# First sequence's heads by products into row groups, and a new deal of the pieces between attention steps

## Chip, cores and metric

The kernel runs on one core of one Trainium2 chip. Its time is the device time of one execution in microseconds, as the median of the runs of one chip.

## What is computed

Eight sequences of 256 tokens with 128 channels pass through five residual blocks, all in fp32. The change touches the end of the first expert block, the attention block, and the start of the second expert block.

```python
x = L0_attn_x                                     # (8, 256, 128)
x = x + 0.5 * _L0_ffn_ref(_layernorm(x), ...)     # 8 experts, 2 for each token
x = x + _L0_attn_ref(_layernorm(x), w_q, w_k, w_v, w_o)
x = x + 0.5 * _L0_ffn_ref(_layernorm(x), ...)     # the same experts again
x = x + 0.5 * _L1_ffn_ref(_layernorm(x), ...)     # channel mix
x = x + _L1_attn_ref(_layernorm(x), ...)          # gated long convolution
x = x + 0.5 * _L1_ffn_ref(_layernorm(x), ...)

# attention: 16 heads of 8 channels, within each sequence
scores = jnp.einsum('bqhd,bkhd->bhqk', q, k) * 8 ** -0.5
weights = jax.nn.softmax(scores, axis=-1)
out = jnp.einsum('bhqk,bkhd->bqhd', weights, v)
concat @ w_o.T

# experts
h = rmsnorm(x @ W_in.T, in_norm_w)
logits = h @ Wr.T                                 # 2 best of 8, softmax over both
out += gates[:, e:e+1] * rmsnorm(silu(h @ Wg[e].T) * (h @ Wu[e].T) @ Wd[e].T, enorm_w[e])
rmsnorm(out, out_norm_w) @ W_out.T
```

## The kernel before

The 2048 tokens lie as four chunks of four tiles of 128 tokens (`xs`); a chunk is two sequences. The kernel has five stages. The first expert stage routes the tokens (`dispatch`), scatters their rows by expert into HBM (`hs`), and `experts` works through 23 groups of 256 rows, whose results GpSimd scatters into `y2`. In the second stage, attention, each chunk's results are first fetched and added to the tokens (`combine`), and the tokens that are done with attention are already routed for the second expert stage (`dispatch` with f=1, in the parts `LATE`: three chunks, then two times two tiles). Then come the second expert stage and a tail with the other three blocks.

The program fixes by hand the order of instructions on TensorE (PE), VectorE (DVE), ScalarE (ACT) and the DMA queue of SyncE (SP): each engine executes what the code issues to it in the order of the code, and waits in place for what an instruction reads. GpSimd (POOL) is not among these four; its order is made when the program is compiled. So a piece of work that is put between two others also stands between them on every engine that it uses.

**Attention steps.** `attention` runs 32 steps s, one for each sequence b and each group g of four heads (`place`: b, g = divmod(s, 4)), and eight more to drain. A head's 8 channels lie on the first 8 of 32 partitions, a row group; four row groups j hold four heads, and `qs` and `ks` (the halves of `qks`, two buffers, by chunk) have a column block for each g. Row 8 of each row group in `ks` is 1, so that the negated maximum of a query, written in row 8 of `qa`, is subtracted by the product itself. A step issues (L947 and on):

- first half: the products `ps` of `weights(s-2, 1)` with `pm` of `scores(s, 0)` side by side; the exponential `es` of the former (ACT, `power`); `turn_top(s-1)`, which transposes the maxima (`pmt`) and adds them to the queries (`qa`, DVE L851); the pieces `first[s]`; the maximum `m` of `scores(s, 0)` (DVE L839)
- second half: `weights(s-1, 0)` with `scores(s, 1)`, exponential, maximum, `average(s-2)` (products `po` of `es` with the values), then the pieces `second[s]`

`weights` takes its bank pair always from `pz`, so a product waits for the exponential before it. The pieces between take the one bank `sa` ("side").

**Pieces of a chunk before its steps.** `mixing` (from `combine` by way of `combined`): `fetch` (SP: two DMAs), `sums` (cf: DVE, power on POOL), `added` (acc: four tiles by DVE for f=0 and by ACT for f=1, four additions on DVE), `turned` (pan; copy and squares on ACT), `produced` (ori: power on POOL; pout), `update` (x, DVE). Then `norm_sums` (statistics on DVE, power on POOL), `norm_rows` (xn_a, DVE L725), `turn_rows` (pxn_a, copy), `to_heads` (pqk for queries, then for keys; after both a DMA of `qkc` to HBM, L747, and four DMAs, one for each j, from there to the rows of `qks`, L750), `values` (pv). `power_of` is L138, `(x) ** -0.5` on POOL.

The prologue runs all of this for chunks 0 and 1, the second two pieces behind the first; only the last two pieces of chunk 1 are dealt to steps 0 and 1. The pieces of chunk c+1 for c = 1, 2 are dealt to the steps o-2 to o+5, with o = 8c.

**Pieces after.** For each sequence `turn_back`, `turn_heads`, `out_heads` (the output projection, added to x). For each part of `LATE` the pieces of `dispatch`: `turned` (pxt), `half0` and `half1` (pin; copy and squares on ACT), `measured`, `normed` (ri: power on POOL; logits lg on DVE L339; rows hrow scaled on ACT L342), two times `choice` (DVE), `places` (prank; DVE), `rows` (two row scatters for each tile on POOL, L399). They are dealt from step o+12 on; the last two parts come in steps 32 to 37. `table` then counts the groups, and the second expert stage's loads follow.

Of the kernel before, what the change touches and what calls it, by code (L numbers as in the profile page):

```python
# [16 lines left out]
P = 128  # L17
# [28 lines left out]
def macaron_kernel(ctx: ExitStack, tc: tile.TileContext, a: dict, out: bass.AP):  # L46
# [59 lines left out]
    for c in range(1, NCH):  # L106
# [10 lines left out]
    idx_col, onehot, rpe_in, rpe_g, rpe_b, onw, wout_t = pack(  # L117
        "pack3", [2, 1, FEAT, LAYERS * FEAT, LAYERS * FEAT, 1, D]
# [24 lines left out]
    def inv_rms(src, dst, name, eps=rms_eps):  # L143

        n = src.shape[1]
        sq = norm.tile([P, n, D], F32, tag="sq", name=f"sq_{name}")
        nc.scalar.activation(sq, src, AF.Square)
        nc.vector.tensor_reduce(dst, sq, AX.X, ALU.add)
        nc.scalar.activation(dst, dst, AF.Sqrt, bias=eps, scale=1.0 / D)
        nc.vector.reciprocal(dst, dst)  # L150

# [131 lines left out]
    def dispatch(f, i, parts, mp):  # L283
# [45 lines left out]
        def normed():  # L329
# [6 lines left out]
            else:  # L336
                power_of(ri, ri, mhalf.to_broadcast([P, nt]))
            st["lg"] = small.tile([P, nt, E], F32, tag="lg", name=f"lg_{n}")
            nc.vector.tensor_mul(st["lg"], st["u"][:, :, D : D + E], bc_last(ri, E))  # L339
            for t in range(nt):  # L340
                u = st["u"][:, t, 0:D].unsqueeze(1).to_broadcast([P, 2, D])
                nc.scalar.activation(hrow[:, t, :, 0:D], u, AF.Copy, scale=ri[:, t : t + 1])  # L342
# [67 lines left out]
        return turned, *halves, measured, normed, *choices, places, rows  # L410
# [173 lines left out]
    def combine(f, c, gates, y2, mp, work=None, half=None):  # L584

        n = f"f{f}_{c}"
        st = {}
        work = work or (lambda tag, name: norm.tile([P, TPC, D], F32, tag={"A": "acc", "B": "at", "C": "sq"}[tag], name=f"{name}_{n}"))
        half = half or (lambda tag, name: bank(f"{name}_{n}", "side"))

        def fetch():
            st["y"] = mp.tile([P, 2, TPC, ROW], F32, tag="y", name=f"y_{n}", bufs=4 if f else 2)
            for k in range(2):
                r = k * NTOK + c * CT
                nc.sync.dma_start(st["y"][:, k], y2[r : r + CT, :].rearrange("(t p) c -> p t c", p=P))

        def sums():
            y = st["y"]
            st["cf"] = small.tile([P, 2, TPC], F32, tag="cf", name=f"cf_{n}")
            nc.vector.tensor_scalar(st["cf"], y[:, :, :, D], 1.0 / D, RMS_EPS, ALU.mult, ALU.add)  # L600
            half = mhalf.unsqueeze(2).to_broadcast([P, 2, TPC])
            power_of(st["cf"], st["cf"], half)

        def added():
            y, cf = st["y"], st["cf"]
            nc.vector.tensor_mul(cf, cf, gates[:, ts(c, TPC), :].rearrange("p t k -> p k t"))
            acc = work("A", "acc")
            for t in range(TPC):
                scale = cf[:, 0, t : t + 1]
                if f:  # L610
                    nc.scalar.activation(acc[:, t], y[:, 0, t, 0:D], AF.Copy, scale=scale)  # L611
                else:
                    nc.vector.tensor_scalar(acc[:, t], y[:, 0, t, 0:D], scale, None, ALU.mult)
            for t in range(TPC):
# [3 lines left out]
            st["acc"] = acc  # L618

        def turned():  # L620
            acc = st["acc"]
            pt = half("a", "pan")
            for t in range(TPC):
                nc.tensor.transpose(pt[:, ts(t, P)], acc[:, t, :], ident)
            st["at"] = work("B", "at").rearrange("p t d -> p (t d)")
            nc.scalar.copy(st["at"], pt)
            st["ss"] = small.tile([P, TPC], F32, tag="ss", name=f"oss_{n}")
            sq = work("C", "osq")
            for t in range(TPC):
                nc.scalar.activation(sq[:, t], acc[:, t], AF.Square, accum_out=st["ss"][:, t : t + 1])  # L630

        def produced():
            ri = small.tile([P, TPC], F32, tag="ri", name=f"ori_{n}")
            nc.vector.tensor_scalar(ri, st["ss"], 1.0 / D, RMS_EPS, ALU.mult, ALU.add)
            power_of(ri, ri, mhalf.to_broadcast([P, TPC]))
            pp = half("b", "pout").rearrange("p (t d) -> p t d", t=TPC)
            for t in range(TPC):
                nc.tensor.matmul(pp[:, t, :], st["at"][:, ts(t, P)], wout_o, start=True, stop=True)
            st["ri"], st["pp"] = ri, pp

        def update():
            x = xs[c]
            for t in range(TPC):
                nc.vector.scalar_tensor_tensor(
                    x[:, t], st["pp"][:, t], st["ri"][:, t : t + 1], x[:, t], ALU.mult, ALU.add
# [26 lines left out]
    def heads(hp):  # L672
# [26 lines left out]
        def attention(mixing, leaving, filter_ends):  # L699
# [5 lines left out]
            with tc.tile_pool(name="at2", bufs=2, reuse_waits="tile") as a2:  # L705
                lns, normed, flat, qkc, osbs, ccs, cts, ess, tops = ({} for _ in range(9))

                def norm_sums(c):
                    x = xs[c]
                    st = small.tile([P, TPC, 6], F32, tag="ast", name=f"ast_{c}")  # L710
                    mv = small.tile([P, TPC, 2], F32, tag="amv", name=f"amv_{c}")
                    for t in range(TPC):
                        nc.vector.bn_stats(st[:, t, :], x[:, t, :])
                    for t in range(TPC):
                        nc.vector.bn_aggr(mv[:, t, :], st[:, t, :])
                    rs = small.tile([P, TPC], F32, tag="ars", name=f"ars_{c}")
                    nc.vector.tensor_scalar(rs, mv[:, :, 1], LN_EPS, None, ALU.add)
                    power_of(rs, rs, mhalf.to_broadcast([P, TPC]))
                    lns[c] = mv, rs

                def norm_rows(c):
                    mv, rs = lns[c]
# [627 lines left out]
```

## Time and profile before

| | us |
|---|---|
| median of three runs (727.02, 730.21, 735.18) | 730.21 |
| profiled execution | 732.74 |
| its span | 731.00 |

| Stretch of the span, us | length | PE busy | ACT busy | DVE busy | granted clock |
|---|---|---|---|---|---|
| 209.67 to 236.15: first combined rows to first scores | 26.48 | 13.92 | 7.13 | 11.43 | 0.65 |
| 236.15 to 246.74: to the first `qa` | 10.59 | 8.19 | 0.59 | 2.45 | 0.50 |
| 246.74 to 284.07: to the eighth `qa` | 37.33 | 31.87 | 15.76 | 22.58 | 0.84 |
| 284.07 to 428.25: to the 32nd `qa` | 144.18 | 122.08 | 75.22 | 96.97 | 0.92 |
| 428.25 to 457.15: to the places of the last two tiles | 28.90 | 18.73 | 8.15 | 11.30 | 0.50 |

Over the whole span PE is busy 574.2 us (79%), DVE 373.3 (51%), ACT 272.7 (37%) and POOL 210.5 (29%). The instruction of `qa` with number k belongs to step k, so the distance between two of them is the length of a step. A row of the timeline gives start, duration, engine, line, operation, the tile written and the tiles read, their shapes and the count; in brackets stands how long the engine was idle before, and what ended that. The granted clock is the share of full speed that TensorE had. Products of 32x256 in the steps last 0.48 us (the first of a group) at clock 1.00 and 0.80 at 0.50.

### The profile page before, as it was taken

How to read it: one execution, taken by the hardware profiler on the slowest of the kernel's cores; microseconds unless marked ns; L12 is line 12 of the kernel's file. 1: busy time of each engine (PE TensorE's matmuls, PEld its weight loads, DVE VectorE, ACT ScalarE, POOL GpSimd, SP SyncE). 2: the span in 40 equal slices, each digit the busy share in tenths (PEclk: the TensorE clock that was granted, in tenths of full speed). 3: DMA queues.
4: the chain of work that ended last, by engine and by line, in shares of the span. 5: the costliest groups of instructions: out<-in, count | busy, mean ns of one | idle time of the engine just before them, and what ended most of it. 6: DMA issues, size and time to landing. Idle time of an engine off the chain costs nothing. (4 is left out here: it accounts for less than half of the span.)

```text
span 731.0 us, 11632 instructions
## 1 busy us (share of the span) xinstructions
PE 574.2 (79%) x4023; PEld 447.7 (61%) x4023; DVE 373.3 (51%) x1109; ACT 272.7 (37%) x664; POOL 210.5 (29%) x217
## 2 busy tenths in 40 slices
PE   3533999999945789998979684199999981779985
PEld 2432988899833445564545343189999971457863
DVE  4661655444343357687557445334444431566564
ACT  3531232223222145574554432022332322765343
POOL 1573456433331001001400442213343343321010
PEclk9999999999966599999999765599999996679998
DMA  5128456666233400030210000756666524000001
GB/s 189 37 82 227 166 181 184 199 195 206 63 87 77 67 2 1 2 59 1 69 21 1 30 30 15 202 160 211 203 196 212 190 62 116 1 0 2 1 14 44
DMA packets 41515, 69.55 MB, mean 95 GB/s; under 512 B 5291, under 2 KB 31698, under 8 KB 41328
## 3 DMA queue, kind: packets, MB, share of 16 engines
q1 hardware_dynamic: 35312, 59.26, 28.1%
q0 software_dynamic: 4992, 8.48, 3.6%
q10 hardware_dynamic: 1152, 1.06, 0.6%
q8 instruction: 32, 0.52, 0.3%
q14 instruction: 27, 0.22, 0.1%
HBM read 55.05 MB, written 15.56 MB: 97 GB/s over the span
## 5 line engine op out<-in xcount | busy, mean ns | idle before, releaser
L555 POOL DMA_INDIRECT y<-yrow_f,idx_f x92 | 90.2, 981 | 160.7 <-issue 153.5
L819 PE MATMUL ps<-qa,qk 32*128 32x256 f32 x512 | 82.2, 443 | 24.1 <-ACT es L856 21.9
L399 POOL DMA_INDIRECT hs<-hrow,posi_f x64 | 61.9, 967 | 109.1 <-issue 48.5
L839 DVE TENSOR_REDUCE m<-pm 128x4 f32<-128x1024 f32 x64 | 77.2, 1220 | 29.2 <-PE pm L802 29.2
L537 PE MATMUL py_f<-w_f,hg_f 128*128 128x128 f32 x736 | 90.2, 276 | 2.4 <-DVE yrow_f L548 2.4
L537 PEld LDWEIGHTS py_f<-w_f,hg_f 128*128 128x128 f32 x736 | 88.6, 192 | 4.9 <-DVE yrow_f L548 2.7
L517 PE MATMUL pg_f<-ht_f,w_f 128*128 128x256 f32 x368 | 90.6, 391 | 1.2 <-issue 0.6
L856 ACT ACTIVATE es<-ps 128x1024 f32<-128x1024 f32 x64 | 65.5, 1023 | 67.2 <-PE pm L802 33.9
L530 DVE TENSOR_TENSOR hg_f<-pu_f,sg_f 128x1024 f32<-128x1024 f32 x46 | 56.3, 1225 | 61.6 <-PE pu_f L526 61.6
L526 PE MATMUL pu_f<-ht_f,w_f 128*128 128x256 f32 x368 | 87.4, 381 | 0.0
L802 PE MATMUL pm<-qk 32*128 32x256 f32 x512 | 81.8, 445 | 7.0 <-DMA qk<-heads 7.0
L819 PEld LDWEIGHTS ps<-qa,qk 32*128 32x128 f32 x512 | 49.4, 206 | 47.0 <-ACT es L856 39.4
L519 ACT ACTIVATE sg_f<-pg_f 128x1024 f32<-128x1024 f32 x46 | 47.1, 1024 | 77.3 <-PE pg_f L517 77.3
L517 PEld LDWEIGHTS pg_f<-ht_f,w_f 128*128 128x128 f32 x368 | 68.7, 197 | 10.0 <-issue 1.0
L526 PEld LDWEIGHTS pu_f<-ht_f,w_f 128*128 128x128 f32 x368 | 66.9, 191 | 7.3
L547 ACT ACTIVATE ysq_f<-py_f 128x128 f32<-128x128 f32 x92 | 24.6, 274 | 122.8 <-PE py_f L537 122.8
L802 PEld LDWEIGHTS pm<-qk 32*128 32x128 f32 x512 | 49.1, 207 | 10.2 <-issue 8.2
L511 DVE TENSOR_SCALAR ht_f<-pht_f,pack 128x256 f32<-128x256 f32 x46 | 22.2, 484 | 50.4 <-PE pht_f L509 50.4
L548 DVE TENSOR_TENSOR yrow_f<-py_f,w_f 128x256 f32<-128x256 f32 x46 | 19.6, 426 | 52.8 <-ACT ysq_f L547 52.8
L509 PE MATMUL pht_f<-ident,hst_f 128*128 128x128 f32 x92 | 18.4, 283 | 31.2 <-DMA hst_f<-hs 31.2
L866 PE MATMUL po<-es,v 128*32 128x256 f32 x512 | 40.1, 428 | 0.1
L138 POOL TENSOR_TENSOR cf_f<-cf_f,mhalf 128x8 f32<-128x8 f32 x8 | 13.1, 1643 | 88.1 <-DVE cf_f L600 88.1
(243 smaller groups left out, 826.2 us busy)
## 6 DMA issues: line engine op xcount, KB each, us to landing
w_f<-in_wall_dram SPq DMA_DIRECT2D x46, 832.0 KB
hst_f<-hs SPq DMA_DIRECT2D x46, 129.0 KB
y_f<-y SPq DMA_DIRECT2D x16, 258.0 KB
heads<-qkc SPq DMA_DIRECT2D x4, 512.0 KB
qk<-heads SPq DMA_DIRECT2D x16, 128.0 KB
pack<-in_pack_dram SPq DMA_DIRECT2D x1, 1729.0 KB
y<-yrow_f,idx_f POOLq DMA_INDIRECT x92, 4.5
hs<-zero ACTq DMA_DIRECT2D x8, 129.0 KB
```

What stands on the lines that cost most here:

```text
L399: ins = nc.gpsimd.indirect_dma_start(out=hs, out_offset=bass.IndirectOffsetOnAxis(ap=st["posi"][:, t, k : k + 1], axis=0), in_=hrow[:, t, ...
L517: nc.tensor.matmul(pg[:, k, :], w[t][:, ts(k, P)], ht[t], start=True, stop=True)
L519: nc.scalar.activation(sg, pg, AF.Silu)
L526: nc.tensor.matmul(pu[:, k, :], w[t][:, DFF + k * P : DFF + k * P + P], ht[t], start=True, stop=True)
L530: nc.vector.tensor_mul(hg[t], pu, sg)
L537: nc.tensor.matmul(py[:, s, :], hg[t][:, k, ts(s, P)], w[t][:, 2 * DFF + k * D : 2 * DFF + k * D + D], start=(k == 0), stop=(k == NFC - 1),)
L555: ins = nc.gpsimd.indirect_dma_start(out=y2, out_offset=bass.IndirectOffsetOnAxis(ap=idx[:, s : s + 1], axis=0), in_=yrow[:, s, :], in_off ...
L802: nc.tensor.matmul(sc[:, jj, i, :], qs[c][r, g, col + i * P : col + (i + 1) * P], ks[c][r, g, col : col + S], start=True, stop=True,)
L819: nc.tensor.matmul(sc[:, jj, i, :], ks[c][r, g, col + i * P : col + (i + 1) * P], tops[s][r, :], start=True, stop=True,)
L839: nc.vector.tensor_reduce(m, sc, AX.X, ALU.max, negate=True)
L856: nc.scalar.activation(es, sc, AF.Exp, scale=scale)
L866: nc.tensor.matmul(po[32 * j : 32 * j + 32, :], vs[c][:, (b % 2) * 2 + i, (g % 2) * (H // 2) + (g // 2) * 4 + j, :], ess[s, j // 2][:, j % ...
```

## The change

1. **First sequence.** The prologue no longer works on chunks 0 and 1, but on the two sequences of chunk 0 (tiles 0, 1 and 2, 3), the second two pieces behind the first. All pieces take a range of tiles. The queries and keys of the first sequence go to no DMA: `heads_of_first(g)` multiplies with the weights' columns from 8g on, so that group g's heads fall on the first 8 rows of each row group, and writes them to `ks` (DVE: times a mask of those rows, plus the row of ones) and to `qs` (ACT: times the mask). Group 0 is made in the prologue, groups 1 to 3 in steps 0 to 2. The second sequence's heads take the DMAs, from step 0.
2. **Chunk 1** is combined, normalized and projected in steps 0 to 6, as the later chunks are in theirs. For all chunks `sums` to `values` now stand in steps o-1 to o+6 instead of o-2 to o+5; both products of `to_heads` stand at the end of step o+5, where they stood in step o+4.
3. **Engines.** The first factor of `added` is scaled on ACT for f=0 too; `norm_rows` goes from DVE to ACT (with an offset computed on DVE).
4. **Routing for the second expert stage.** `normed` is split into `normed` (power), `logits` and `scaled`, which can be dealt apart; all pieces are dealt out anew, and those of the last two parts stand in steps 32 to 34. The first expert stage and the tail issue what they issued.

```diff
-        return turned, *halves, measured, normed, *choices, places, rows
+        if f == 0:
+            return turned, *halves, measured, both(normed, logits, scaled), *choices, places, rows
+        return turned, *halves, measured, normed, logits, scaled, *choices, places, rows
...
-                if f:
-                    nc.scalar.activation(acc[:, t], y[:, 0, t, 0:D], AF.Copy, scale=scale)
-                else:
-                    nc.vector.tensor_scalar(acc[:, t], y[:, 0, t, 0:D], scale, None, ALU.mult)
+            for t in own:
+                nc.scalar.activation(acc[:, t], y[:, 0, t, 0:D], AF.Copy, scale=cf[:, 0, t : t + 1])
...
+                def heads_of_first(g):
+                    m = P - HD * g
+                    pp = bank(f"pqk1_{g}", "side").rearrange("p (i s) -> p i s", i=2)
+                    for i in range(2):
+                        w = (wq_t, wk_t)[i][:, HD * g : P]
+                        nc.tensor.matmul(pp[0:m, i, :], w, flat[0, 0][:, 0:S], start=True, stop=True)
+                    nc.vector.tensor_scalar(
+                        ks[0][0:m, g, 0:S], pp[0:m, 1, :], lanes8[0:m], onehot[0:m], ALU.mult, ALU.add
+                    )
+                    nc.scalar.activation(qs[0][0:m, g, 0:S], pp[0:m, 0, :], AF.Copy, scale=lanes8[0:m])
...
                     if c < NCH - 2:
+                        n = c + 1
                         at(o + 12, None, turned)
-                        at(o + 13, None, half0, measured)
-                        at(o + 15, None, half1)
-                        at(o + 16, None, None, normed_)
-                        at(o + 18, None, choice0)
-                        at(o + 19, None, choice1)
-                        at(o + 20, None, None, places)
+                        at(o + 13, None, half0)
+                        at(o + 14, half1, measured)
+                        at(o + 15, None, normed_)
+                        at(o + 16, None, logits)
+                        at(o + 17, None, choices[0], partial(scaled, [0, 1]))
+                        at(o + 19, None, partial(scaled, [2, 3]))
+                        at(o + (20 if n < NCH - 2 else 18), None, choices[1])
+                        at(o + (21 if n < NCH - 2 else 19), None, places)
                         for i in range(TPC):
-                            at(o + 21 + i, None, partial(rows, [i]))
+                            at(o + (21 if n < NCH - 2 else 20) + i, None, partial(rows, [i]))
                     elif c == NCH - 2:
-                        at(o + 12, turned, half0, measured)
-                        at(o + 13, half1, None, normed_)
-                        at(o + 14, None, choice0)
-                        at(o + 15, None, choice1, places, rows)
+                        at(o + 12, None, turned)
+                        at(o + 13, half0, half1, measured)
+                        at(o + 14, normed_)
+                        at(o + 15, logits, choices[0])
+                        at(o + 16, choices[1], scaled)
+                        at(o + 17, places, rows)
                     else:
...
+                        at(o + 8, turned, half0, half1, measured, normed_)
+                        at(o + 9, logits, scaled, choices[0])
...
-                    if 1 <= c < NCH - 1:
+                    if c < NCH - 1:
                         n = c + 1
-                        sums, added, turned, produced, update = mixing[n]
-                        at(o - 2, None, None, sums)
-                        at(o - 1, None, None, added)
-                        at(o, turned, produced)
-                        at(o + 1, update, partial(norm_sums, n))
-                        at(o + 2, None, partial(norm_rows, n))
-                        at(o + 3, None, partial(turn_rows, n))
-                        at(o + 4, partial(to_heads, n, 0), partial(to_heads, n, 1))
-                        at(o + 5, partial(values, n), None)
+                        sums, added, turned, produced, update = mixing[n + 1]
+                        at(o - 1 if c else 0, sums if not c else None, sums if c else None)
+                        at(o, None, added)
+                        at(o + 1, turned, produced)
+                        at(o + 2, update)
+                        at(o + 3, None, partial(norm_sums, n))
+                        at(o + 4, None, partial(norm_rows, n))
+                        at(o + 5, partial(turn_rows, n), partial(to_heads, n))
+                        at(o + 6, None, partial(values, n))
...
+                for g in range(1, 4):
+                    at(g - 1, partial(heads_of_first, g), None)
                 for i, step in enumerate(ahead[1][-lag:]):
                     at(i, step, None)
```

`at(s, one, two, ...)` puts `one` in `first[s]` and the rest in `second[s]`. Within one list the pieces stand in the order of the calls. The pieces of step 34 follow one another at its end: the seventh sequence's output projection and both last parts of the routing, down to their `rows`.

## The prediction

> **What bounds the kernel now.** I read the busy-tenths table, then the stretch before the attention stage, its steps, and the waits. The edits lie between 209.7 us (first combined rows land) and 457.2 us (last rows of the second expert stage get places). What runs before and after keeps its instructions, so the sum is a shift of the 457.2 us point.
>
> The timeline of all engines, from the prologue's last products to the first scores:
>
> ```profile
> 224.06 3.78 PE L741 MATMUL pqk<-xnt_a,pack 128*128 128x512 f32 x4 [0.68 <-ACT xnt_a L735]
> ...
> 228.49 0.33 SPq L747 DMA_DIRECT2D heads<-qkc  x1
> ...
> 231.17 2.96 SPq L750 DMA_DIRECT2D qk<-heads  x4
> 236.12 0.49 PEld L802 LDWEIGHTS pm<-qk 32*128 32x128 f32 x2 [6.70 <-issue]
> 236.15 1.19 PE L802 MATMUL pm<-qk 32*128 32x256 f32 x2 [5.90 <-DMA qk<-heads]
> 238.45 1.35 PEld L802 LDWEIGHTS pm<-qk 32*128 32x128 f32 x6 [1.84 <-DMA qk<-heads]
> 238.45 2.07 PE L802 MATMUL pm<-qk 32*128 32x256 f32 x6 [1.12 <-DMA qk<-heads]
> ```
>
> The round trip through HBM ends last: 228.49 to 236.15, TensorE idle for 5.90 and 1.12 us. The last product ran at half rate, as these stretches say (after start, end and length: PE, PEld, DVE, ACT, POOL busy; then granted clock, DMA share, GB/s):
>
> ```profile
> 226.00:228.00 2.00, 2.00 (x5) 0.86 (x4) 1.11 (x4) 0.70 (x2) 0.24 (x1) 0.50 0.00 0
> 228.00:230.00 2.00, 2.00 (x14) 1.42 (x12) 0.00 (x0) 1.62 (x4) 0.00 (x0) 0.99 0.36 145
> ...
> 256.00:258.00 2.00, 2.00 (x24) 0.82 (x20) 0.96 (x1) 1.02 (x1) 0.00 (x0) 0.50 0.00 0
> 258.00:260.00 2.00, 2.00 (x26) 0.90 (x18) 0.26 (x1) 0.07 (x1) 0.00 (x0) 0.81 0.00 0
> ```
>
> [...]
>
> Inside the steps the chain is: weights, exponential, weights, exponential, since both halves use one bank pair (pz). Undisturbed (exponentials at 264.56, 266.88, 269.19 us) a step takes 4.63 us, 2 x (1.02 exponential + 1.07 products + handing over); TensorE works some 4.0 us of it. The 31 steps from the first `qa` (246.74) to the 32nd (428.25) take 181.5 us, 38 us over that. The longest stall, in the timeline:
>
> ```profile
> 408.54 0.96 POOL L399 DMA_INDIRECT hs<-hrow,posi_f  x1 [0.30 <-issue]
> 409.52 1.04 POOL L138 TENSOR_TENSOR ri_f<-ri_f,mhalf 128x4 f32<-128x4 f32 x1
> 410.60 0.19 DVE L339 TENSOR_TENSOR lg_f<-u_f,ri_f 128x32 f32<-128x32 f32 x1 [5.65 <-POOL ri_f L138]
> 410.60 1.71 ACT L342 ACTIVATE hrow<-u_f,ri_f 128x256 f32<-128x256 f32 x4 [5.44 <-POOL ri_f L138]
> ...
> 413.26 0.80 PE L819 MATMUL ps<-qa,qk 32*128 32x256 f32 x2 [6.70 <-ACT es L856]
> ```
>
> The power for chunk 2's rows stands on GpSimd behind seven row scatters of 1.26 us each; ScalarE and VectorE wait for it in front of the exponential and `qa`; TensorE idles 6.70 us and returns at half rate (0.80 for 0.48 us).
>
> **The change, part by part.**
>
> *A. To the first scores.* The first sequence (two tiles) goes alone; its heads come from products into their row groups, with no DMA. From 209.67 us, each handing-over 0.05 to 0.25: power of 4 values 1.0 (row `ori_f`, 1.01) to 211.0; product with gates to 211.2; two scalings on ScalarE at 0.31 spacing to 211.9; two adds at 0.28 to 212.65; two half-rate transposes 0.6 to 213.2; copy 0.37 to 213.7; two squares with readout at 0.5 to 214.7; scalar 0.17, power 0.73 to 215.9; two updates to 216.5; statistics 0.48, 0.30, 0.17 to 217.4; power to 218.4; offset 0.17, two normalizations 0.48 and 0.41 to 219.6; transposes to 220.2; copy to 220.8; four passes over 256 columns at half rate, 4 x 0.48, to 222.7; the two copies out of PSUM to 223.3. That copy on VectorE is nearest to `ht_f` (0.48), on ScalarE to `ct` (0.37). In TensorE's order the second sequence's transposes precede the scores, behind its normalizations (0.9) and 0.6: scores at 224.8. If ScalarE, which alternates between both sequences, delays the first by its squares once more, it is 226.8. The first pair of row fetches is half as large; I count no earlier landing (up to 1 us). **-11.4 us** (-9.4 to -12.4).
>
> *B. Steps 0 to 7* (236.15 to 284.07). Chunk 1's combining, normalization and heads move into these steps. At full clock TensorE gets 0.66 + 1.16 + 0.66 + 2.04 + 1.06 = 5.6 us (rows `pan`, `pout`, `pxn_a`, `pqk`, `pv` of chunk 2), 2.0 for row groups 2 and 3 and 0.5 for the second sequence's values: +8.1, counted whole although a step leaves TensorE 0.6 us. On SP the second sequence's five DMAs now stand before chunk 3's fetch, which has until step 15; on GpSimd chunk 1's three powers (1.63, 1.01, 1.01) meet nothing else before step 7. Step 0: 2.07 scores, 1.02 heads, 0.65 wait for the side bank, 1.02 second sequence's heads, 1.2 scores, 1.22 maximum, 1.0 chunk 1's adds ahead of `qa`, 0.7: 8.9 for 10.59, -1.7. TensorE works almost unbroken from 220.8, so I take full clock from step 0's second half, as after 224 to 228; then the excess of steps 1 and 2 (7.55 and 6.01 against 4.63: 4.3) goes. **+2.1 us**; with half rate until step 2, as now, step 0 at 11.0 and 2.0 of the 4.3 gone: +0.4 + 8.1 - 2.0 = +6.5.
>
> *C. Steps 8 to 31* (284.07 to 428.25). Splitting `normed` lets ScalarE scale rows a step or two after the power, two tiles at a time, and chunk 1's scatters start a step earlier. The function used brings no table load: the tail uses it (`xn_m`) and the last load is at 463.65. From one `qa` to the next, steps 17, 25 and 29 to 31 took 6.76, 7.65, 9.05, 9.30, 8.25; I take 5.8, 5.3 and three of 5.6: -1.0 - 2.3 - 9.8 = -13.1. Against it: (i) both head products of a chunk now stand at the end of one step on the single side bank, behind `half0`: 0.73 + 1.02 + 1.02 of products with copies 0.39 and 0.59 and two squares between, about +2.5 in step 13; step 21, with places too, replaces step 20 (10.0) at about +0.6; (ii) normalization and scaling on ScalarE, 1.65 and 1.25, against its gap of 1.29 between exponentials: 0.4 each, four times, +1.6 (VectorE is freed of 1.11 and 0.87; below nothing if `qa` gains from that); (iii) heads have two steps instead of three to return. From `heads` issue to the second landing is 10.0 us (228.49 to 238.45), to the end of transfers 12; two steps less 0.9 give 9.3, a stall of 0.7, three times: +2.1; hidden it is 0. Sum **-6.3 us** (-13.1 to +6).
>
> [...] The rows have 0.48 alone and 0.41 in a run (`xn_m`), against 1.11 for four on VectorE (`xn_a`). [...]
>
> *D. The end* (428.25 to 457.15). GpSimd sets it: chunk 2's scatters can start some 8.2 us after the last `qa` (4.5 of products at full clock, places 1.5 + 1.9), last 10.1, four more 5.05, then power, choices and places of the last two tiles as now, 0.73 + 0.25 + 5.5: 29.9 against 28.90. **+1.0 us**; -3.4 if the last power is put before those four; +4 at half rate.
>
> Sum: -11.4 + 2.1 - 6.3 + 1.0 = -14.6. The profiled execution (732.74, span 731.00) would take 718.1; from the median 730.21, 2.5 lower, **716**.
>
> [...]
>
> **The rivals.**
> 1. *Nothing given back* (C's -13.1 whole): -21.4, 709. For: TensorE's work between 284 and 428 is 122 of 144 us and hardly changes. Against: step 20 shows what three users of one side bank cost.
> 2. *The round trip is exposed in each chunk*: all four lanes needed (12 - 9.3 = 2.7) plus a clock dip of 2 us, as after the 2.69 us idle before 380.35 (0.64 for 0.38), three times 4.7, 12 more than counted: -2.6, 728. For: 12 us seen twice. Against: half the lanes are needed half a step later.
> 3. *Slower: half rate lasts.* If step 0's small waits keep TensorE at half rate through step 7, steps 3 to 7 cost 2.95 more each (14.8) and chunk 1's pieces 5.6: B is 6.5 + 20.4, the sum +10.2, 740. It decides from the middle of step 5 (each step costs 4.1 of the 10.2 that B at 6.5 leaves as gain); slower by over 1% from step 7. For: half rate from 236 to 258 at 70 to 90% work. Against: 224 to 228.
> 4. *The first sequence doesn't go ahead*, because the second's pieces hold its engines: A shrinks to -9.4, within the forecast.
>
> **How the numbers follow.** Forecast 0.53, rival 1 0.20, rival 2 0.15, rival 3 0.12. 1% of 730 is 7.3 us, about what can be told from no change. Faster: 0.53 + 0.20 = 0.73 (the forecast's own range, with the ends of A, B and D but not all at once, is 709 to 723); same 0.15; slower 0.12. The range goes from 709 less D's 4.4 (704) to 728 plus D's 3 (731) and leaves out rival 3.
>
> **What would show it.** Right: no wait of first scores on `qk<-heads`, scores near 225; full clock before step 2; no idle over 2 us on TensorE from the wait of `hrow` for `ri_f`; step 20 or 21 still near 10 us. Wrong: TensorE waiting on `qk<-heads` before steps 8, 16 or 24; clock 0.5 beyond 245 us; scatters before a power that ScalarE waits for.

## The result and the profile after

Over 20 runs of each kernel on one chip the changed kernel takes 729.48 us (723.91 to 733.88) and the kernel before 728.82: ratio 1.0004, 95% interval 0.9979 to 1.0029. No change, where 14 us of gain were forecast. The profiled execution of the changed kernel takes 732.56 us, its span is 730.8.

Both kernels were profiled once more on another chip (runs x7 and x7b below). By the stretches of the prediction, in us, before and changed:

| stretch | first chip | second chip | forecast | measured, first and second chip |
|---|---|---|---|---|
| A: y rows to first scores | 26.48, 14.10 | 26.49, 13.97 | -11.4 | -12.4, -12.5 |
| B, steps 0 to 2 | 24.15, 29.44 | 20.86, 25.20 | | +5.3, +4.3 |
| B, steps 3 to 7 | 23.78, 28.08 | 23.77, 28.08 | | +4.3, +4.3 |
| B together | 47.93, 57.51 | 44.62, 53.28 | +2.1 | +9.6, +8.7 |
| C: 8th to 32nd `qa` | 144.18, 141.35 | 140.98, 147.31 | -6.3 | -2.8, +6.3 |
| D: to the last places | 28.73, 29.26 | 28.73, 29.13 | +1.0 | +0.5, +0.4 |
| all of it | 247.32, 242.23 | 240.83, 243.69 | -14.6 | -5.1, +2.9 |

Ahead of the y rows the changed kernel is 3.2 us later on the first chip and 1.2 us earlier on the second; behind the last places it takes 1.7 more and 1.5 less. Apart from the fetch of the y rows no instruction there was edited, and the signs differ, so I take it for difference between executions. One profile of each kernel on a chip is therefore good to a few us only; the 20 runs of each say that the change is worth nothing.

The way to the first scores is as forecast. The timeline of the changed kernel, from the products to the second half of step 0:

```profile
222.62 2.08 PE L799 MATMUL pqk<-xnt_a,pack 128*128 128x256 f32 x4 [0.46 <-ACT xnt_a L765]
...
227.01 2.08 PE L856 MATMUL pm<-qk 32*128 32x256 f32 x8
...
229.02 2.06 PE L799 MATMUL pqk<-xnt_a,pack 128*120 128x256 f32 x4
231.12 0.54 DVE L800 TENSOR_SCALAR qk<-pqk,pack 120x256 f32<-120x256 f32 x1 [5.69 <-PE pqk L799]
...
231.70 0.47 ACT L803 ACTIVATE qk<-pqk,pack 120x256 f32<-120x256 f32 x1 [4.21 <-DVE qk L800]
232.23 2.08 PE L779 MATMUL pqk<-xnt_a,pack 128*128 128x256 f32 x4 [1.15 <-ACT qk L803]
234.23 2.10 PE L856 MATMUL pm<-qk 32*128 32x256 f32 x16
```

The first scores follow the products with no transfer between. The loss starts right behind them: the second sequence's products (232.23) need the side bank, which group 1's products hold until both copies are out; the copy on ScalarE waits for the one on VectorE, and TensorE idles 1.15 us. In step 1 TensorE waits twice more for a copy to free the bank (0.68 and 1.14 us), and in step 2 once for the `update` that frees it (1.55 us):

```profile
240.60 2.05 PE L799 MATMUL pqk<-xnt_a,pack 128*112 128x256 f32 x4 [0.68 <-ACT at_f L647]
...
243.79 1.22 PE L809 MATMUL pv<-pack,xnt_a 128*128 128x128 f32 x4 [1.14 <-ACT qk L803]
...
251.53 1.11 PE L799 MATMUL pqk<-xnt_a,pack 128*104 128x256 f32 x4 [1.55 <-DVE x L665]
```

The clock, in the windows of the same profile (start, end and length: PE, PEld, DVE, ACT, POOL busy; clock, DMA share, GB/s):

```profile
228.00:230.00 2.00, 2.00 (x8) 1.14 (x5) 0.00 (x0) 0.00 (x0) 0.00 (x0) 0.50 0.00 0
...
246.00:248.00 2.00, 2.00 (x17) 1.35 (x10) 0.87 (x1) 0.93 (x1) 0.00 (x0) 0.54 0.00 0
248.00:250.00 2.00, 1.98 (x23) 1.26 (x22) 0.43 (x2) 0.45 (x2) 1.01 (x1) 1.00 0.01 4
```

TensorE works at half rate until 247.9, through step 0 and most of step 1 (it ends at 250.02).

The stall of the kernel before at steps 29 to 31 is gone: those steps take 14.28 us, which were 26.59. For the same chunk 2 the changed timeline has the power, the logits and the rows apart:

```profile
417.30 1.04 POOL L138 TENSOR_TENSOR ri_f<-ri_f,mhalf 128x4 f32<-128x4 f32 x1 [1.91 <-DVE ri_f L338]
...
421.69 0.18 DVE L349 TENSOR_TENSOR lg_f<-u_f,ri_f 128x32 f32<-128x32 f32 x1
...
428.79 1.69 ACT L354 ACTIVATE hrow<-u_f,ri_f 128x256 f32<-128x256 f32 x4
```

The power no longer stands behind scatters (GpSimd waits for its input), the rows are scaled 10.5 us after it, and nobody waits. What was gained there is paid in steps 13 and 14 (9.78 became 16.52, the same within 0.01 us in all three profiles of the changed kernel) and 20 to 22 (19.78 became 23.62). In the kernel before, the two products of the heads lie a half step apart, and `half0` comes a step later:

```profile
303.69 1.02 PE L741 MATMUL pqk<-xnt_a,pack 128*128 128x512 f32 x2
...
308.07 1.12 PE L741 MATMUL pqk<-xnt_a,pack 128*128 128x512 f32 x2 [0.68 <-ACT xnt_f L297]
...
313.54 0.73 PE L317 MATMUL pin_f<-win_r,xnt_f 128*128 128x136 f32 x4
```

Step 13's end in the changed timeline:

```profile
315.89 0.73 PE L324 MATMUL pin_f<-win_r,xnt_f 128*128 128x136 f32 x4
316.66 0.39 ACT L328 COPY u_f<-pin_f 128x272 f32<-128x272 f32 x1
...
317.10 1.13 PE L779 MATMUL pqk<-xnt_a,pack 128*128 128x512 f32 x2 [0.47 <-ACT u_f L328]
...
318.26 0.58 ACT L781 COPY qkc<-pqk 128x512 f32<-128x512 f32 x1 [0.49 <-PE pqk L779]
...
318.90 1.12 PE L779 MATMUL pqk<-xnt_a,pack 128*128 128x512 f32 x2 [0.68 <-ACT qkc L781]
319.97 0.48 PE L856 MATMUL pm<-qk 32*128 32x256 f32 x2
```

Three users of one bank in turn: between 315.89 and the next step's scores at 319.97 lie 2.98 us of products and 1.15 of waits for copies (they overlap a little), with no attention product between them.

### The profile page after: what moved, and what is told of

The parts are those of the page before. It is cut to its first block, busy times and chain, and to the rows that moved or that the text cites. A ratio compares the mean times of both kernels' runs of the same rounds, so it can differ in the third digit from the quotient of the medians.

```text
span 730.8 us, 11703 instructions
## 1 busy us (share of the span) xinstructions
PE 572.7 (78%) x4039; PEld 447.8 (61%) x4039; DVE 368.7 (50%) x1090; ACT 284.2 (39%) x703; POOL 211.6 (29%) x220
## 5 line engine op out<-in xcount | busy, mean ns | idle before, releaser
L540 PE MATMUL pu_f<-ht_f,w_f 128*128 128x256 f32 x368 | 89.3, 387 | 0.0
L873 PE MATMUL ps<-qa,qk 32*128 32x256 f32 x512 | 74.2, 406 | 16.4 <-ACT es L910 15.3
L856 PE MATMUL pm<-qk 32*128 32x256 f32 x512 | 76.2, 417 | 1.1 <-DMA qk<-heads 1.0
L873 PEld LDWEIGHTS ps<-qa,qk 32*128 32x128 f32 x512 | 43.9, 186 | 35.3 <-ACT es L910 28.5
L856 PEld LDWEIGHTS pm<-qk 32*128 32x128 f32 x512 | 45.9, 192 | 3.6 <-DMA qk<-heads 2.3
L523 PEld LDWEIGHTS pht_f<-ident,hst_f 128*128 128x128 f32 x92 | 13.2, 147 | 39.0 <-DMA hst_f<-hs 17.5
L905 DVE TENSOR_TENSOR qa<-pmt,qk 128x256 f32<-128x256 f32 x32 | 13.5, 423 | 44.3 <-PE pmt L899 44.0
```

Of the source, the lines that this page charges most:

```text
L523: nc.tensor.transpose(pt[:, ts(s, P)], hst[t][:, s, 0:D], ident)
L540: nc.tensor.matmul(pu[:, k, :], w[t][:, DFF + k * P : DFF + k * P + P], ht[t], start=True, stop=True)
L856: nc.tensor.matmul(sc[:, jj, i, :], qs[c][r, g, col + i * P : col + (i + 1) * P], ks[c][r, g, col : col + S], start=True, stop=True,)
L873: nc.tensor.matmul(sc[:, jj, i, :], ks[c][r, g, col + i * P : col + (i + 1) * P], tops[s][r, :], start=True, stop=True,)
```

## The experiments

Theory: the gain of A and of steps 29 to 31 is real, and the pieces' queue on the one side bank gives it back. Rivals: the half rate does it; the moved work does it wherever it stands; the products are worth nothing. The chips differ: the kernel before takes near 729 us on two of them and 746 to 748 on three, so runs are compared by their ratio to it and by stretches on one kind of chip. In the table, A, 0-2 (steps), 3-7 and C are the stretches above in us, each from one profile; before and this are medians.

| run | before, us | this, us | ratio (95%) | A | 0-2 | 3-7 | C |
|---|---|---|---|---|---|---|---|
| x7 changed | 729.1 | 728.4 | 0.998 (0.995-1.002) | 13.97 | 25.20 | 28.08 | 147.31 |
| x7b before | 729.1 | 728.4 (one run) | | 26.49 | 20.86 | 23.77 | 140.98 |
| x9 | 729.1 | 728.9 | 1.001 (0.997-1.004) | 18.75 | 21.86 | 28.15 | 142.22 |
| x6 | 729.1 | 709.4 | 0.974 (0.968-0.979) | 14.11 | 20.10 | 25.80 | 136.28 |
| x1 | 748.4 | 746.3 | 0.997 (0.994-1.000) | 27.10 | 20.26 | 23.77 | 149.66 |
| x3 | 748.4 | 740.1 | 0.988 (0.985-0.992) | 13.97 | 26.53 | 25.83 | 148.54 |
| x4 | 748.4 | 744.7 | 0.994 (0.992-0.997) | 13.21 | 26.96 | 28.08 | 153.96 |
| x5 | 748.4 | 737.9 | 0.983 (0.979-0.987) | 13.97 | 17.72 | 28.21 | 154.34 |
| x10 | 747.5 | 740.5 | 0.989 (0.987-0.992) | 19.02 | 21.27 | 26.46 | 149.29 |
| x11 | 747.5 | 732.5 | 0.981 (0.979-0.983) | 13.23 | 19.15 | 25.91 | 147.49 |
| x13 | 747.5 | 729.8 | 0.977 (0.975-0.978) | 13.97 | 18.06 | 25.49 | 146.91 |
| x1 again | 747.5 | 746.9 | 0.999 (0.997-1.001) | 26.82 | 20.16 | 23.77 | 149.08 |
| y1 changed | 747.4 | 746.6 | 0.999 (0.996-1.002) | 13.96 | 26.53 | 28.08 | 153.05 |
| y2 = x6 | 747.4 | 731.0 | 0.979 (0.974-0.984) | 13.97 | 17.72 | 25.82 | 150.50 |
| y3 = x10 | 747.4 | 739.1 | 0.987 (0.983-0.990) | 19.09 | 21.37 | 26.26 | 149.45 |
| y4 | 747.4 | 726.5 | 0.971 (0.967-0.975) | 13.29 | 19.43 | 24.64 | 144.02 |
| z1 = x1 | 746.3 | 743.6 | 0.996 (0.993-0.999) | 26.99 | 23.55 | 23.78 | 149.30 |
| z2 before | 746.3 | 748.1 (one run) | | 26.69 | 20.59 | 23.76 | 147.94 |

**The two kernels again.** x7, x7b and y1 change nothing.

> The changed kernel as it is, profiled again beside the others. [...] The stop of some 7 us at steps 28 and 29 that all four kernels of the first job show: if it belongs to the chip, it is there too; if to their edits, it is not. Its time against before: 0.995 to 1.005 if this chip weighs both kernels as the first did.

> The kernel before as it is, profiled again beside the others, for the parts of its time on this chip: y rows to first scores 26 to 27.5 us, first scores to 8th qa 43 to 48, 8th to 32nd qa 143 to 152, and steps 29 to 31 at 25 to 28 us if POOL's order (the scatters of one part ahead of the power that the next part's rows wait for) makes them, less if it was chance.

> The changed kernel as it is, on one chip with the three runs beside it. If this chip is like the first job's and the third's (before near 748 us) it tells whether the stop of some 7 us at step 28 is there without any edit of mine: step 28 at 10.4 and 29 at 7.3 to 7.7 us; on a chip like the others (before near 729) 5.0 and 5.1. Its time against before 0.995 to 1.005 on either.

Steps 0 and 1 took 8.53 and 10.24 us in x7, 8.54 and 11.56 in y1, 12.31 and 10.70 in the first profile. The clock differs (the eight first scores take 1.13 us in y1, 2.08 in the first profile), the loss stays. Steps 29 to 31 of the kernel before are 26.57 us again. The stop at step 28 is in y1 and not in x7: it goes with the chip (last section).

**Two side banks in steps 0 and 1** (x5). `sb` is free until the first average in step 2.

```diff
-                turn["side"] = ("sa",)
+                turn["side"] = ("sa", "sb")
...
                 for s in range(last + 8):
+                    if s == 2:
+                        turn["side"] = ("sa",)
```

> The changed kernel with two side banks in turn (sa and sb, which is free until the first average) in steps 0 and 1. Theory W (copies out of the one side bank hold TensorE): the waits of 1.15, 0.68 and 1.14 us on ACT copies go, steps 0 and 1 fall by 2.5 to 4 us together, the whole kernel 725 to 727.5. Rival C (the half rate alone): TensorE's work is the same, the steps fall by less than 1 us, the whole kernel 728.5 to 730.5.

Its timeline, for the stretch shown above:

```profile
231.48 1.13 PE L856 MATMUL pm<-qk 32*128 32x256 f32 x8
...
232.54 1.12 PE L799 MATMUL pqk<-xnt_a,pack 128*120 128x256 f32 x4
233.50 1.03 PE L779 MATMUL pqk<-xnt_a,pack 128*128 128x256 f32 x4
233.71 0.55 DVE L800 TENSOR_SCALAR qk<-pqk,pack 120x256 f32<-120x256 f32 x1 [3.66 <-PE pqk L799]
...
234.29 0.48 ACT L803 ACTIVATE qk<-pqk,pack 120x256 f32<-120x256 f32 x1 [2.33 <-DVE qk L800]
234.46 2.20 PE L856 MATMUL pm<-qk 32*128 32x256 f32 x16
```

The copies still run one after the other, but TensorE no longer waits for them. Steps 0 to 2 take 17.72 us against 26.53 of y1 on a like chip, 8.8 less; steps 0 and 1 alone take 7.4 less, where 2.5 to 4 were expected of the waits: without them the clock stays up too (step 1's products take 1.03 us at 238.90, where they took 2.05 in the changed profile at 240.60).

**One user of the side bank in each half step** (x3), and both edits (x6, y2).

```diff
-                        at(o + 12, None, turned)
-                        at(o + 13, None, half0)
+                        at(o + 11, None, turned)
+                        at(o + 12, half0)
...
-                        at(o + 4, None, partial(norm_rows, n))
-                        at(o + 5, partial(turn_rows, n), partial(to_heads, n))
-                        at(o + 6, None, partial(values, n))
+                        at(o + 4, partial(norm_rows, n), partial(turn_rows, n))
+                        at(o + 5, partial(to_heads, n, parts=(0,)), partial(to_heads, n, parts=(1,)))
+                        at(o + 7, None, partial(values, n))
```

> The changed kernel with one user of the side bank in each half step, where it has up to three: norm_rows in the first half of step o+4, turn_rows in its second half, the queries' product in the first half of o+5, the keys' in the second, values in o+7; of the later pieces turned in o+11 and half0 in the first half of o+12. Theory S (the pieces that queue on the single side bank at a step's end make steps 5, 6, 13, 14, 21, 22 long): steps 5+6 fall from 14.2 to about 10, 13+14 from 16.5 to about 11, 21+22 from 18.7 to about 13, the heads reach their rows some 1 to 2 us earlier, the whole kernel 714 to 719. Rival F (it is the sheer work of TensorE and ScalarE that those steps carry, wherever it is put): the time moves to steps 4, 7, 11, 12, and the whole stays at 727 to 731.

> The edits of x3_spread and x5_two_banks together in the changed kernel: two side banks in steps 0 and 1, and one user of the side bank in each half step from step 4 on. Theory S+W (the two losses are separate and add up): steps 0 to 2 near 7, 6 and 5 us as in x5, steps 5+6, 13+14 and 21+22 near 10, 11 and 16 as in x3, first scores to 32nd qa some 6 to 8 us below x5's 200.3 us; the whole 0.970 to 0.976 of the kernel before. Rival (the loss only moves, since TensorE's order has no room elsewhere): within 2 us of x5, that is 0.981 to 0.985.

> x6_spread_two_banks on the same chip as the changed kernel. Theory S+W (the pieces' queue on the one side bank is what gave the gain back): 17 to 21 us below the changed kernel in the same job, steps 0 to 2 some 5 to 8 us shorter in all, 5+6, 13+14 and 21+22 some 4, 5 and 5 us shorter. Rival (part of the 0.974 was the chip): less than 14 us below it.

The same instructions, dealt otherwise: steps 5+6 fall from 14.22 to 10.21 us, 13+14 from 16.52 to 11.36, in x3, x6 and y2 alike; 21+22 fall from 18.65 (first profile) to 12.95 in x6, the one such run on a chip near 729 us. In y2's timeline the two products of step 13 lie a half step apart, and neither waits for a copy:

```profile
303.76 1.02 PE L781 MATMUL pqk<-xnt_a,pack 128*128 128x512 f32 x2
304.82 0.59 ACT L783 COPY qkc<-pqk 128x512 f32<-128x512 f32 x1 [0.21 <-PE pqk L781]
306.79 1.13 PE L781 MATMUL pqk<-xnt_a,pack 128*128 128x512 f32 x2
```

x6 is 19 us below the changed kernel on one chip, y2 15.6 on another (17 to 21 were expected). That is the gain that the prediction had promised of the change, and more. Stretch by stretch, x6 against x7b on the same chip gives A -12.4, B +1.3, C -4.7 and D +0.4, together -15.4 us, where the prediction had -11.4, +2.1, -6.3 and +1.0, together -14.6. Of it, x3's part is paid back a little at step 8 (6.4 to 7.6 us in x6), where the heads now arrive later.

**The clock** (x4: idle products of the identity in front of the first scores; x11: the same in x6). They add products that no result uses.

```diff
+                fill(16, bank("warm0", "sb"))
                 for step in filter_ends:
                     step()
+                warm = bank("warm1", "sb")
+                fill(12, warm)
```

> The changed kernel with idle 128x128 products of the identity, read by nobody, put on TensorE before the filter's last products (16), after them (12), and one after each piece of the prologue (about 18), so that TensorE is nearly always busy from 204 to 227 us. Theory C (the half rate up to 248 us is what lengthens steps 0 to 2): clock 1.00 from before the first scores; step 0 falls from 12.3 to 8 or 9 us and step 1 from 10.7 to 7.5 or 8, the time to the first scores stays within 1 us, the whole kernel 720 to 724. Rival W (steps 0 to 2 are set by copies out of the one side bank and by waits on VectorE): they fall by 3 us together at most, and the fillers cost up to 1 us ahead of the first scores: 726 to 730.

> x6_spread_two_banks with the idle products of x4_warm ahead of the first scores. Theory C (what is left of the clock's part is the half rate up to 228 us): full rate throughout, step 0 falls from 9.5 to about 7.2, y rows to first scores from 14.1 to some 13.2, the whole 2.5 to 3.5 us below x6, 0.969 to 0.971. Rival (steps 0 to 2 wait for copies and DVE whatever the rate): within 1 us of x6.

In x4 the clock is full when the first scores start, and falls all the same (windows as above):

```profile
228.00:230.00 2.00, 1.99 (x14) 1.69 (x13) 0.69 (x3) 0.51 (x2) 1.00 (x2) 1.00 0.00 0
...
240.00:242.00 2.00, 1.32 (x5) 0.69 (x5) 0.21 (x1) 1.70 (x9) 0.00 (x0) 0.92 0.22 66
242.00:244.00 2.00, 0.85 (x3) 0.54 (x3) 1.65 (x2) 0.54 (x2) 0.00 (x0) 0.50 0.69 97
```

Step 0 takes 8.54 us, as in y1, where the first scores ran at full rate without fillers (1.13 us for eight), and in x7; the clock falls between 240 and 242 us, around the end of step 0, where TensorE is busy for 2.70 of 4.00 us from 238 to 242, and steps 0 to 2 are no shorter than in y1. So a warm start did not save these steps: with the queue on the bank the half rate came back. How much of the loss is the waits and how much the rate that follows them is not separated; x5 removed both. By its ratio x4 gains some 3.6 us against y1 on another chip (the two intervals just overlap); where is not clear from its stretches. x11 has no x6 beside it on its chip; against y2 on another its steps 0 to 2 are no shorter (19.15 and 17.72), so nothing more can be said of fillers in x6.

**The products against the round trip** (x9 in the changed kernel; x10 and y3 in x6).

```diff
-                        partial(heads_of_first, 0) if i == 0 else partial(to_heads, 0, seqs[i]),
+                        partial(to_heads, 0, seqs[i]),
...
-                for g in range(1, 4):
-                    at(g - 1, partial(heads_of_first, g), None)
```

> The changed kernel with the first sequence's queries and keys by the round trip through HBM (one heads DMA and four qk DMAs) in place of the four products and their masked copies; all else as changed. Theory P (the products shorten the way to the first scores by the round trip): y rows to first scores 14.1 becomes 18.5 to 20.5, and steps 0 to 2 lose three pairs of products and copies, 1 to 2 us each at half rate, so the whole is 0 to 4 us longer than the changed kernel. Rival G (the products give back in steps 0 to 2 all that they gain): the whole is equal to the changed kernel within 1.5 us, or shorter.

> x6_spread_two_banks with the first sequence's queries and keys by the round trip through HBM in place of the products (as x9 does in the changed kernel, where it cost nothing). Theory P2 (the products' gain ahead of the first scores, 14.0 against 18.75 us, was given back only because heads 1 to 3 queued on the one side bank in steps 0 to 2; with two banks it is kept): steps 0 to 2 differ by less than 1.5 us in all, and the whole is 3 to 5 us longer than x6, 0.978 to 0.981 of the kernel before. Rival (the products' work in steps 0 to 2 costs what they gain, whatever the bank): equal to x6 within 1.5 us, 0.972 to 0.976.

> x10 again (x6 with the first sequence's heads by the round trip), now on one chip with x6. Theory P2 (with two banks the products keep their gain): 3 to 7 us above x6 in the same job. Rival (the products give back in steps 0 to 2 what they gain, as in the changed kernel): within 1.5 us of x6.

In the changed kernel the products gain 4.8 us to the first scores and lose 3.3 in steps 0 to 2, and the medians are equal: there the products are worth nothing. (The first sequence's going ahead alone, which x9 keeps, takes A from 26.5 to 18.75.) With the bank free they gain 5.1 and another 3.7 in steps 0 to 2, where less than 1.5 was expected (after 5.37 us of idling for `qk<-heads` y3's products stay at half rate up to 252.2 us), and the median is 8.1 us lower, 731.0 against 739.1 on one chip.

**The deal alone** (x1, x1 again, z1: the kernel before with the new `leaving` part and the split `normed`).

```diff
-                        at(o + 16, None, None, normed_)
-                        at(o + 18, None, choice0)
...
+                        at(o + 15, None, normed_)
+                        at(o + 16, None, logits)
+                        at(o + 17, None, choices[0], partial(scaled, [0, 1]))
...
```

> The kernel before with the new deal of the later pieces alone (dispatch cut into normed, logits and scaled, and the `leaving` part of the hand-made order); prologue, heads and mixing pieces as before. Theory D (the deal's gain at steps 29 to 31 is real and independent of the prologue; the long steps 13, 14, 21, 22 of the changed kernel come from turn_rows and to_heads one step later on the same side bank): steps 29 to 31 fall from 26.6 us to some 14.5, steps 13+14 stay near 10, 8th to 32nd qa falls from 144.2 to 130 to 134, the whole kernel 717 to 721. Rival E (the deal itself makes the long steps, by half0 and half1 where the queue has no room): 13+14 and 21+22 lengthen as in the changed kernel by some 6.8 and 3.8, the whole kernel 725 to 730.

> x1_deal_only once more, since all four kernels of the first job stopped for some 7 us at steps 28 and 29, which hides the deal's worth. Theory D (the deal's gain at steps 29 to 31 is real): no stop here, 8th to 32nd qa at 130 to 136 us against 141 to 144 of the kernel before, the whole 0.984 to 0.990. Rival E (what it gains at the end it pays in steps 14 to 23, where x1 already showed 14, 18, 21 and 22 longer than before): 0.994 to 1.001.

> x1_deal_only with the kernel before profiled on the same chip. Theory D' (the deal is worth its 10 to 12 us at steps 29 to 31 and pays some of it in steps 10, 14, 18 to 22): on a chip where the kernel before takes near 729 us, 8th to 32nd qa 4 to 8 us below the kernel before and the whole 0.988 to 0.995; on one where it takes near 747 us, the deal meets the stop at steps 28 and 29 in whole and the kernel before in part, and the whole is 0.996 to 1.000 as twice before. Rival E (the deal gains nothing on either): 0.997 to 1.002 on a 729 us chip too.

> The kernel before for its parts on this chip. On a 747 us chip: if TensorE is held while GpSimd issues a part's scatters whatever the order of the pieces, one or two steps between 20 and 31 are 3 to 8 us longer than on the first chip, and the way to the first expert stage takes 8 us more as in all runs there; on a 729 us chip steps 29 to 31 at 26 to 27 us again.

Against z2 on the same chip, z1 has steps 29 to 31 8.3 us and 20 to 22 2.9 us shorter, step 10 1.6, 13+14 1.3, 15 to 19 3.0 and 23 to 28 6.7 longer. On these chips TensorE stops in the middle of a part's scatters, in z2 at step 21 (10.45 us, which is 5.07 on the first chip), in the deal at 28 and 29 (10.25 and 7.75). So the deal moves its gain into a stop that such a chip adds; the three ratios say 0.1 to 0.4% (the intervals of two reach 1.000). What it is worth alone on a 729 us chip was not measured.

**Earlier heads, and the best version** (x13: x6 with the heads earlier and `half0` to `normed` later; y4: x13 with the fillers of x4).

```diff
-                        at(o + 3, None, partial(norm_sums, n))
-                        at(o + 4, partial(norm_rows, n), partial(turn_rows, n))
-                        at(o + 5, partial(to_heads, n, parts=(0,)), partial(to_heads, n, parts=(1,)))
-                        at(o + 7, None, partial(values, n))
+                        at(o + 2, None, partial(norm_sums, n))
+                        at(o + 3, None, partial(norm_rows, n))
+                        at(o + 4, partial(turn_rows, n), partial(to_heads, n, parts=(0,)))
+                        at(o + 5, partial(to_heads, n, parts=(1,)))
+                        at(o + 8, partial(values, n))
```

> x6_spread_two_banks with the next chunk's statistics, rows and heads half a step to a step earlier (norm_sums in o+2, norm_rows in o+3, turn_rows and the queries' product in o+4, the keys' in the first half of o+5), values in o+8, and half0, measured, half1, normed in o+13, 14, 15, 16. Theory R (the round trip still ends after its steps' start: 3.1 us of TensorE waiting in step 8 of x6 and a fall of the clock for 3.4 us): steps 8, 16, 24 fall from 7.6, 6.2, 5.5 to about 5.4, 5.4, 4.6, no wait for qk<-heads, the whole 3 to 5 us below x6, 0.967 to 0.970. Rival (the moved pieces cost as much in steps 13 to 16): within 1.5 us of x6.

> x13 and x11 together: two side banks, one user of a bank in each half step, the heads half a step to a step earlier, and idle products that keep TensorE busy ahead of the first scores. Theory: full clock in steps 0 to 2 in every execution and no wait for the round trip; 3 to 7 us below x6 in the same job. Rival (the rest of x6 hides both): within 1.5 us of x6.

Step 8 falls from 7.74 us (y2) to 6.56 (x13) and 5.21 (y4), 13+14 to 9.75, as before the change. x13's ratio, 0.977, misses the expected 0.967 to 0.970 and cannot be told from the 0.979 of y2; TensorE still waits 0.99 us for the heads before step 8. y4 is 4.5 us below y2 on one chip, as expected. Of the two reasons given, one shows: no wait for `qk<-heads` is left. The other does not: at the end of step 0 the clock falls (the products of 237.34 take 1.91 us, in y2 1.03; full rate is back before the scores of 240.41, 0.38 us), and steps 0 to 2 take 1.7 us more than in y2. y4 beats both kernels: 726.5 against 747.4 and 746.6 us, ratio 0.971.

Not tried: the change's prologue with the old deal, since there `turn_back` would ask for the bank ahead of the `update` that frees it; the moves to ScalarE by themselves; and the two edits of x6 in the kernel before, so that how much of x6's gain needs the change is known from the stretches alone.

## Why the prediction was wrong, by its steps

**A** was right: no wait on `qk<-heads`, -12.4 and -12.5 us, at the end of its range.

**B is the step that failed.** It priced the side bank at one wait of 0.65 us and took full clock from step 0's second half. It added durations of rows, +8.1 for the moved pieces, and took off 6.0 for step 0 and the clock: +2.1. Measured: +9.6 and +8.7. What costs is the queue: product, copy on VectorE, copy on ScalarE, next product, each link in TensorE's own order, so that the scores behind wait too; and then the clock. TensorE waited for the bank 1.15 us in step 0, 1.82 in step 1 and 1.55 in step 2, and steps 5 and 6 take 14.2 us where they took 9.4. The moved work itself costs little: with banks to spare, steps 1 to 7 take 36.4 us (y2) where the kernel before has 34.3 on a like chip (z2), and step 0 gives 2.9 back. So that x6 comes near the forecast of B is partly luck, since two terms were too large and offset each other: +8.1 for the moved work, and -4.3 for the excess of steps 1 and 2, which belonged to that one execution (x7b has 1.1 there).

Full clock from step 0's second half was my estimate from the stretch 224 to 228, and no run of the changed kernel shows it. The profile that it was read from speaks against it: from 238.45 to 244.74 us TensorE was busy for 6.28 of 6.29 us, and the granted clock stayed at 0.50. In the first profile of the changed kernel full clock came at 247.9 us; in y1 it came ahead of the first scores (1.13 us for eight at 231.91) and was gone in step 1 (2.05 us for the products at 241.69). What I didn't weigh is a second bank: in x5, with two in turn, the second sequence's products (233.50) start before the copies of group 1's (233.71 and 234.29), and three steps are 8.8 us shorter.

**C** had its gain right and one giveback far too small, for the same reason as in B; on the second chip it missed by more than B (+6.3 for -6.3). Steps 29 to 31 gave 12.3 us, forecast 9.8. Giveback (i), two products at one step's end, was +2.5 in step 13 and +0.6 for steps 20 and 21; measured +6.7 in 13+14 and +3.8 in 20 to 22 (+11.1 in x7). Its rows were the right rows, but 0.73 + 1.02 + 1.02 and three copies at a step's end are not hidden by the 0.6 us that a step leaves TensorE, and `half1`, `turn_back` and `values` queue behind them in step 14. Step 25 gained 3.0 us, but 26 and 27 lost 3.4. Giveback (iii), the round trip, was forecast at 2.1 and came near it: steps 8, 16 and 24 took 1.6 us more together, 0.9 in x7. (ii) was not measured apart.

**D** was right (+0.5), and so was its path: chunk 2's scatters start 8.1 us after the last `qa` (433.97 after 425.88), forecast 8.2.

**Rivals.** The first fell with giveback (i). The second fell too: TensorE waits for `qk<-heads` only 1.0 us in all (0.61 before step 8, 0.44 before step 24), so that its 728 lies near the measured time is luck. The third had the sign of B and named the wrong mover: the half rate did last beyond 245 us, which the prediction had set as its own mark of error, but in x4 a warm clock (1.00 up to 240 us) didn't hold over those waits (0.50 from 242).

## What to carry to other kernels

Price a piece that is dealt between steps not by its rows but by the chain that its buffer makes: with one PSUM bank, each user cost here product, copies and handing over, in the order of the engine that everyone needs (group 1's in step 0: 2.06 us, then 0.54 and 0.47, and TensorE idle for 1.15). Before a deal is judged, list the users of each bank by half step; an idle bank and a half step's distance together gave here 16 to 19 us for the same instructions. And waits on TensorE cost here more than their own length: the 8.8 us that x5 takes off steps 0 to 2 had been some 4.5 us of waits for the bank.

## What the runs showed of the hardware

**The clock does not follow busy time alone.** In the changed profile TensorE works without a break from 227.01 to 231.08 and from 232.23 to 236.33 us (4.07 and 4.10), and the granted clock stays at 0.50 from 206.89 to 247.85. In the profile before it stays at 0.50 over the 6.28 us of work from 238.45, and rises at 258.77, after 3.91 us without a break. In y1 the two transposes of 231.27 already run at full rate (0.71 us, where the two of 226.35 take 0.86), though TensorE had idled for 0.67, 0.46 and 0.68 us in the 5.6 before. What decides it was not shown; steps 0 and 1 took 18.8 to 23.0 us in three profiles of the changed kernel.

**Two engines' copies out of one PSUM bank ran one after the other.** The masked copies of `pqk` write different halves of `qk`, yet ScalarE's starts 0.03 us after VectorE's ends, four times of four in the changed profile (231.70 after 231.67). No run here shows whether it is the bank or the shared tile `qk` that orders these two copies.

**TensorE stopped while GpSimd issued scatters, on some chips.** On the three chips where the kernel before takes 746 to 748 us the first expert stage starts some 8 us later (73.6 to 75.7 us against 66.4 to 67.5), and the timeline of y1 has this in step 28:

```profile
417.17 0.44 PE L899 MATMUL pmt<-ident,m 128*128 128x128 f32 x2
...
420.47 0.96 POOL L411 DMA_INDIRECT hs<-hrow,posi_f  x1 [0.30 <-issue]
422.91 1.02 ACT L910 ACTIVATE es<-ps 128x1024 f32<-128x1024 f32 x1 [3.75 <-remote]
422.93 0.42 DVE L905 TENSOR_TENSOR qa<-pmt,qk 128x256 f32<-128x256 f32 x1 [7.04 <-remote]
```

`qa` needs only the transposes recorded at 417.17, and starts 5.3 us after their end, behind the seventh of a run of scatters ("remote": no recorded instruction ended the wait); TensorE idles for 4.04 us up to 423.99. On the other two chips the changed kernel's step 28 takes 4.98 us; in all ten runs of the changed kernel and its variants on the three it takes 10.1 to 10.4. The cause stays open.
